# Layer 0 of a four-layer graph network: engine order from a list of steps run through at build time, far entries scaled on ScalarE

## Chip, cores, metric

One core of a Trainium2 chip runs the whole program in one launch. The metric is device time in microseconds (us). The engines are named as in the profile: PE (TensorE, with PEld for its weight loads), DVE (VectorE), ACT (ScalarE), POOL (GpSimd), SP (SyncE, which here only issues transfers).

## The reference, cut to what matters

Four graph layers run one after the other on 2708 nodes with 128 features, each with a residual and a normalisation. The change concerns layer 0 only.

```
# node_feats: x [2708,128]; adj [2708,2708], about 64 entries per row not zero, in 0.05..1
s = x @ msg_w[:, :128].T
d = x @ msg_w[:, 128:].T
messages   = gelu(s[:, None, :] + d[None, :, :] + msg_b)      # exact gelu
aggregated = einsum('ijd,ij->id', messages, adj)
new = concat([x, aggregated]) @ upd_w.T + upd_b
h   = gelu(new) + x
x   = layernorm(x + (layernorm(h) * ln_w + ln_b))
# layers 1 to 3 follow, each a layernorm(x + layer(x, adj))
```

The gelu of a pair (i, j) is wanted only where `adj[i, j]` is not zero. The kernel computes it at those places alone.

## The kernel before, in words

**Tiles and blocks.** The 2708 rows are taken in 22 row tiles (`LT`) of 125 rows (`LR`, five groups of `RG` = 25). For each tile the 2708 columns are 22 blocks (`NB`) of 124 columns (`JB`). So there are 484 blocks, and a block is the unit in which everything is ordered.

**A block.** `begin` (L953) puts the rows' s into the PSUM buffer `sl`, for two blocks at a time. `pick` (L960, ten matmuls) adds, for each row and each of five slots, the d of one neighbour in this block; the same matmul brings that neighbour's adjacency value. A slot matrix `S` (one in the place of the neighbour that has this rank in its row and block) makes the choice. `CAP` = 5 slots hold the first five entries of a row in a block. ACT takes the gelu into `g` (L1042), DVE spreads the adjacency values into `W` (`weigh`, L1026), and `add_up` (L977) multiplies `W` by `g` into the PSUM buffer `acc`. There are three `sl`, six `g` and six `W`.

**Preparing a tile.** For each third of the columns: SP loads the adjacency transposed (`at`, L808/L811), DVE makes a mask (`find`, L817), PE ranks (L825) and ACT casts the ranks (L826); ACT and DVE split the adjacency values into two FP16 parts `dA` (L833, L838), and DVE writes five slots (`slot`, L845).

**Far entries.** A row may have more than five entries in a block. Those past the cap are called far, at most `OV` = 16 a row. SP loads the adjacency by rows (`ar`, L860). PE ranks along rows (L866); DVE keeps the entries past the cap in `o` (`past`, L877), counts them (L879), takes the eight largest of every two blocks (L884) and of those the sixteen largest `v` (L890, L892). FIND_INDEX8 (`where`, L915) finds their columns, twice eight. SP fills a buffer `far` of 128x8x128 with the rows' s, 512 KB (`start_far`, L910); POOL gathers onto it the d of one column per row, eight times (`fetch`, L919, an indirect transfer that adds). ACT takes the gelu of the buffer (`far_gelu`, L925). DVE sums the sixteen with their values, one after the other (`far_sum`, L931, then fifteen of L933). `turn` (L939 to L942, PE) adds this to the tile's sums, `close` (L945, ACT) stores it. There are three `far` buffers. `check` (L899 to L906, eight small DVE operations a tile) compares the count of entries past the cap with the number of values found, and looks for equal values, [...]; a total ends up in an output.

**Order.** Within this stage the order of each engine's instructions is the order in which the program issues them. It is written out by hand: `preparation` and `Rows.when` (from L753) name for every step the block after which it comes, the list of steps is sorted by block, and one loop over the 484 blocks (L1032 to L1053) issues the steps between the blocks. For the far part these lines say it:

```
b = base + NB
yield b, self.largest
yield b + 6, self.check
for n in range(OV // 8):
    yield b + 1 + n * 2, lambda n=n: self.where(n)
...
    yield b - 1 + n * 9, lambda n=n: self.start_far(n)
    yield b + 2 + n * 9, lambda n=n: self.fetch(n)
    yield b + 15 + n * 13, lambda n=n: self.far_gelu(n)
    for k in range(8):
        yield b + 17 + n * 13 + k // 2, lambda n=n, k=k: self.far_sum(n * 8 + k)
yield b + 36, self.turn
yield b + 36, self.close
```

Here `b` is the first block of the tile. An engine takes its instructions in that order and waits on semaphores for what others make. Buffers come from tile pools, so a buffer's next use waits for the last use of the one before. After the last block (L1056 to L1094) the update of the features follows, with the rest of the last tile's far entries between its groups.

Of the kernel before, what the change touches and what calls it, by code (L numbers as in the profile page):

```python
# [14 lines left out]
F32 = mybir.dt.float32  # L15
# [7 lines left out]
P = 128  # L23
# [47 lines left out]
class Step:  # L71


    def __init__(self, engine, cost, emit, after, rank, group, ahead, table, cells, bank, then):
        self.engine, self.cost, self.emit, self.after, self.rank = engine, cost, emit, after, rank
        self.group, self.ahead, self.table, self.cells, self.bank, self.then = group, ahead, table, cells, bank, then
        self.end = None

# [94 lines left out]
def gnn_stack(ctx: ExitStack, tc: tile.TileContext, t, out: bass.AP):  # L173
# [378 lines left out]
    with ExitStack() as l0:  # L552
# [10 lines left out]
        with ExitStack() as msg:  # L563
# [28 lines left out]
            nc.vector.memset(spread, 0.0)  # L592
# [4 lines left out]
            nc.vector.tensor_copy(spread[:, :, :RG], ident[:, :LR].rearrange("p (c i) -> p c i", c=NC))  # L597

            bad = mp.tile([P, LT], F32, name="bad")
# [3 lines left out]
            with tc.tile_pool(name="pre0", bufs=1) as pp:  # L603
                trif = pp.tile([JB, P], F32, name="trif")
                nc.vector.memset(trif, 1.0)
                nc.gpsimd.affine_select(
                    out=trif[:, :JB], in_=trif[:, :JB], compare_op=ALU.is_gt, fill=0.0, base=0,
                    pattern=[[1, JB]], channel_multiplier=-1)
                nc.vector.scalar_tensor_tensor(
                    trif[:, :JB], ident[:JB, :JB], EDGE, trif[:, :JB], op0=ALU.mult, op1=ALU.add)  # L610
                nc.vector.tensor_copy(tri, trif)


# [11 lines left out]
            lp = msg.enter_context(tc.tile_pool(name="load", bufs=3))  # L625
            ap_ = msg.enter_context(tc.tile_pool(name="rowsof", bufs=3))
            mk = msg.enter_context(tc.tile_pool(name="masks", bufs=2))
            sp = msg.enter_context(tc.tile_pool(name="ranks", bufs=3))
            op_ = msg.enter_context(tc.tile_pool(name="past", bufs=1))
            gp = msg.enter_context(tc.tile_pool(name="fetch", bufs=3))  # L630
            vp = msg.enter_context(tc.tile_pool(name="values", bufs=3))
            up = msg.enter_context(tc.tile_pool(name="sums", bufs=2))
            ep = msg.enter_context(tc.tile_pool(name="slots", bufs=6))
            p_misc = msg.enter_context(tc.tile_pool(name="ps_misc", bufs=1, space=PSUM))
            p_slot = msg.enter_context(tc.tile_pool(name="ps_slot", bufs=1, space=PSUM))
            p_out = msg.enter_context(tc.tile_pool(name="ps_out", bufs=1, space=PSUM))
            sl_all = [p_slot.tile([P, 2, BANK], F32, name=f"sl{n}") for n in range(3)]
            for v in sl_all:
                nc.vector.memset(v, 0.0)
# [7 lines left out]
            xT = aggT  # L647

            def turn_x():
                for n, (a, b) in enumerate(spans(0, NT, 4)):  # L650
                    ps = sl_all[n % 3][:, n // 3, :]
                    for i in range(a, b):
                        r = rows[i]
                        nc.tensor.transpose(ps[:, (i - a) * P:(i - a) * P + r], x[:r, i, :], ident[:r, :r])
                    w = min(b * P, N) - a * P
                    (nc.scalar.copy if n % 2 else nc.vector.tensor_copy)(xT[:, a * P:a * P + w], ps[:, :w])

            class Piece:


                def __init__(self, n):
                    self.n = n
                    self.b0, self.b1 = 4 * n, min(4 * n + 4, NB)
                    self.a0, self.a1 = 4 * n, min(4 * n + 4, NT)

                def products(self):
                    b0, b1, a0, a1 = self.b0, self.b1, self.a0, self.a1
                    psd, pss = (sl_all[(2 * self.n + k) % 3][:, 0, :].rearrange("p (b d) -> p b d", d=D)
                                for k in range(2))
                    d = self.d = ep.tile([P, NC, D], F32, name="g")[:JB, :b1 - b0, :]  # L670
                    room = gp.tile([P, 8, D], F32, name="far")
                    s = self.s = room[:, :a1 - a0, :]
                    parts = room[:, 4:, :].rearrange("p i d -> p (i d)").bitcast(FP16)
                    self.parts = parts.rearrange("p (q i d) -> p q i d", q=2, d=D)[:, :, :a1 - a0, :]
                    if N < b1 * JB:
                        nc.vector.memset(d, 0.0)
                    if N < a1 * P:
                        nc.vector.memset(s, 0.0)
                    for b in range(b0, b1):
                        r = min(JB, N - b * JB)  # L680
                        nc.tensor.matmul(psd[:r, b - b0, :], xT[:, b * JB:b * JB + r], msg_d, start=True, stop=True)
                    for i in range(a0, a1):
                        nc.tensor.matmul(pss[:rows[i], i - a0, :], xT[:, i * P:i * P + rows[i]], msg_s,
                                         start=True, stop=True)
                    full = min(b1, NFB) - b0
# [4 lines left out]
                    self.hi, self.lo = (v[:, b0:b1, :, :D] for v in dA)  # L690
                    nc.scalar.activation(self.hi[:, :, 0, :], d, AF.Copy, scale=D_SCALE)
                    self.spread(self.hi)
                    for a, b, r in groups():
                        if a0 <= a < a1:
                            nc.vector.tensor_tensor(s[:r, a - a0:b - a0, :], pss[:r, a - a0:b - a0, :],
                                                    over_tiles(msg_br, b - a, r), op=ALU.add)
                    nc.scalar.activation(self.parts[:, 0], s, AF.Copy, scale=D_SCALE)
                    nc.sync.dma_start(out=s_tab[a0 * P:a1 * P, :].rearrange("(n p) d -> p n d", p=P), in_=s)
# [4 lines left out]
                def spread(self, v):  # L703

                    nc.gpsimd.tensor_copy(v[:, :, 1:, :], v[:, :, 0:1, :].to_broadcast(
                        [JB, self.b1 - self.b0, NC - 1, D]))

                def update(self):
                    ps = p_out.tile([P, PB, D], F32, name="acc")
                    u = ep.tile([P, NC, D], F32, name="g")[:, :self.a1 - self.a0, :]  # L710
                    if N < self.a1 * P:
                        nc.vector.memset(u, 0.0)
                    for a, b, r in groups():
                        if self.a0 <= a < self.a1:
                            for i in range(a, b):
                                nc.tensor.matmul(ps[:r, i - self.a0, :], xT[:, i * P:i * P + r], upd_x,
                                                 start=True, stop=True)
                            nc.vector.tensor_tensor(u[:r, a - self.a0:b - self.a0, :],
                                                    ps[:r, a - self.a0:b - self.a0, :],
                                                    over_tiles(upd_b, b - a, r), op=ALU.add)  # L720
                    nc.sync.dma_start(out=u_tab[self.a0 * P:self.a1 * P, :].rearrange("(n p) d -> p n d", p=P), in_=u)

                def rests(self):
                    b0, b1, a0, a1 = self.b0, self.b1, self.a0, self.a1
                    lo = self.lo
                    nc.vector.scalar_tensor_tensor(self.parts[:, 1], self.s, D_SCALE, self.parts[:, 0], op0=ALU.mult,
                                                   op1=ALU.subtract)
                    nc.vector.scalar_tensor_tensor(lo[:, :, 0, :], self.d, D_SCALE, self.hi[:, :, 0, :], op0=ALU.mult,
                                                   op1=ALU.subtract)
                    self.spread(lo)  # L730
                    for q in range(2):
                        nc.sync.dma_start(out=sq_tab[q, a0 * P:a1 * P, :].rearrange("(n p) d -> p n d", p=P),
                                          in_=self.parts[:, q])

            def preparation():
                yield -NB - 9, turn_x
                for n, b in enumerate((-26, -22, -14, -10, -6, -2)):
                    piece = Piece(n)
                    yield b, piece.products
                    yield b + 2, piece.update  # L740
# [1219 lines left out]
```

## Time and profile before

| | |
|---|---|
| median of 3 runs | 1880.69 us (1878.36 to 1881.56) |
| the profiled execution's own time | 1879.03 us |
| span in the profile | 1877.3 us |
| mean granted TensorE clock | 0.920 |
| layer 0: first gelu of a block, last one | 55.5 us, 855.7 us |
| end of layer 0 | about 897.5 us |
| one row tile in the middle | 36.03 to 36.05 us |

The times of the runs are device times of whole executions. Everything with a line number, a window or an engine comes from the one profiled execution. A row of the groups reads: line, engine, operation, written tile, read tiles, shapes, count, then busy us in all, mean ns of one, and the idle time before it with what ended it. A row of waits reads: who waited, for whom, us in total, times, longest us. In a timeline the columns are start, duration, engine, line, operation, and in brackets the idle time before it.

### The profile page before, as it was taken

Reading aid. Unit: us, or ns where it says so; the run is one execution under the profiler, and the core shown is the slowest. Engines: PE = TensorE matmul, PEld = TensorE weight load, DVE = VectorE, ACT = ScalarE, POOL = GpSimd, SP = SyncE. Lnnn points to the kernel's source line nnn. Section 1 sums busy time; section 2 is a strip of 40 time slices with the busy share of each in tenths; the row PEclk is TensorE's granted clock in tenths of the full one; section 3 lists DMA queues with packets and bytes.
Section 4 is the critical chain, followed back from the end, with each engine's and each line's share of the span. In section 5 each row is a group of like instructions: output and inputs, shape, how many; then the busy total and the mean of one; then the engine's idle time right before and its main releaser. Section 6 shows DMA issues by size and latency. Waiting matters only on the chain.

```text
span 1877.3 us, 36661 instructions
## 1 busy us (share of the span) xinstructions
PE 1581.1 (84%) x14033; PEld 921.2 (49%) x14033; DVE 1432.4 (76%) x3609; ACT 999.4 (53%) x1538; POOL 653.2 (35%) x429
## 2 busy tenths in 40 slices
PE   4889999999999999884799995568888897299995
PEld 4666666666666666663444442312322343044542
DVE  7899999999999999976588885748886782860104
ACT  3556666666666666544344443568886862430003
POOL 5667767777777776664100000010000100000000
PEclk9899999999999999997899998658997798599998
DMA  8757666666666766543044410032333554354431
GB/s 223 167 117 153 127 144 145 135 145 128 147 135 137 151 129 139 101 104 104 0 154 161 164 64 1 9 118 89 139 139 117 171 174 169 118 207 148 148 123 32
DMA packets 234895, 238.29 MB, mean 127 GB/s; under 512 B 28844, under 2 KB 219630, under 8 KB 228122
## 3 DMA queue, kind: packets, MB, share of 16 engines
q1 hardware_dynamic: 183670, 212.18, 36.2%
q0 software_dynamic: 51040, 23.68, 10.6%
q8 instruction: 112, 1.84, 0.4%
q14 instruction: 73, 0.60, 0.1%
HBM read 220.65 MB, written 15.15 MB: 126 GB/s over the span
## 4 chain that ended last, share of the span: by engine, by line
PE 38%; DVE 7%; ACT 6%; issue 1%; DMA 0%; ACTq 0%; DVEq 0%
PE acc L1857 11%; PE lg L1245 5%; PE acc L1252 5%; PE accV L1585 5%; PE ps L1513 4%; PE accO L1589 2%; PE ps L1568 1%; ACT arena L1519 1%; DVE arena L1547 1%; PE ps L1514 1%; ACT x L379 1%; DVE arena L1571 1%; PE ps L447 1%; PE ps_w L1213 1%; ACT arena L1540 0%
## 5 line engine op out<-in xcount | busy, mean ns | idle before, releaser
L919 POOL DMA_INDIRECT far<-d_tab,ix x352 | 583.1, 1657 | 217.3 <-issue 97.0
L1042 ACT ACTIVATE g<-sl 128x640 f32<-128x640 f32 x484 | 335.4, 703 | 297.3 <-PE sl L960 272.5
L960 PE MATMUL sl<-dA,S 124*128 124x153 f16 x4840 | 380.9, 233 | 0.0
L960 PEld LDWEIGHTS <-S 124*128 124x128 f16 x4840 | 326.0, 98 | 72.0 <-issue 69.8
L977 PE MATMUL acc<-g,W 128*32 128x128 f32 x4840 | 194.5, 280 | 15.5 <-DVE W L1026 13.5
L953 PE MATMUL sl<-s,same 50*128 50x459 f16 x968 | 150.5, 333 | 17.8 <-DVE W L1026 15.5
L977 PEld LDWEIGHTS acc<-g,W 128*32 128x32 f32 x4840 | 117.4, 109 | 70.4 <-DVE W L1026 27.5
L1026 DVE TENSOR_TENSOR W<-sl,own 128x125 f32<-128x125 f32 x484 | 131.2, 275 | 21.6 <-ACT g L1042 21.6
L1500 POOL TENSOR_TENSOR arena<-arena,off 128x128 f32<-128x128 f32 (+1 forms) x22 | 23.0, 1049 | 350.3 <-DMA arena<-in_adjT 245.1
L845 DVE TENSOR_SCALAR S<-rk 124x1000 f16<-124x1000 bf16 (+1 forms) x330 | 141.4, 455 | 0.0
L1246 ACT ACTIVATE w<-lg,row_L_gnn_gate_bias 128x512 f32<-128x512 f32 (+1 forms) x132 | 83.4, 636 | 108.2 <-PE lg L1245 107.0
L915 DVE FIND_INDEX8 ix<-v,o 128x8 uint32<-128x2728 f32 x44 | 131.8, 2994 | 0.0
L1585 PE MATMUL accV<-arena,X 128*128 128x512 f32 (+4 forms) x264 | 123.3, 587 | 6.5 <-DVE arena L1551 6.5
L1245 PE MATMUL lg<-qT,mT 128*128 128x512 f32 (+2 forms) x264 | 121.2, 548 | 3.6 <-ACT w L1246 3.1
L1252 PE MATMUL acc<-w,both 128*128 128x512 f32 (+2 forms) x264 | 121.2, 547 | 0.0
L449 DVE TENSOR_TENSOR g<-ps,row_L_gnn_b 128x512 f32<-128x512 f32 (+2 forms) x14 | 7.9, 573 | 147.4 <-PE ps L447 147.3
L933 DVE SCALAR_TENSOR_TENSOR extra<-far,v,extra 128x128 f32<-128x128 f32 x330 | 114.6, 347 | 6.8 <-ACT far L925 0.5
L1513 PE MATMUL ps<-XT 128*128 128x512 f32 (+8 forms) x150 | 91.0, 696 | 32.2 <-ACT arena L1519 26.5
L1857 PE MATMUL acc<-at,x 128*128 128x512 f32 (+2 forms) x156 | 66.2, 575 | 48.5 <-ACT x L379 48.5
L1247 DVE TENSOR_TENSOR w<-w,at 128x512 f32<-128x512 f32 (+1 forms) x132 | 82.6, 626 | 27.1 <-ACT w L1246 27.0
L877 DVE SCALAR_TENSOR_TENSOR o<-ps,ar 128x496 f32<-128x496 f32 x132 | 82.0, 621 | 12.2 <-DMA ar<-in_adj 6.8
L884 DVE MAX8 cand<-o 128x8 f32<-128x248 f32 x242 | 90.4, 412 | 0.0
(359 smaller groups left out, 2494.2 us busy)
## 6 DMA issues: line engine op xcount, KB each, us to landing
at<-in_adjT SPq DMA_DIRECT2D x42, 1354.0 KB
ar<-in_adj SPq DMA_DIRECT2D x105, 248.0 KB
far<-s_tab SPq DMA_DIRECT2D x44, 512.0 KB
at<-in_adjT SPq DMA_DIRECT2D x42, 448.0 KB
arena<-in_adjT SPq DMA_DIRECT2D x21, 704.0 KB
arena<-in_adjT SPq DMA_DIRECT2D x21, 650.0 KB
held<-in_adjT SPq DMA_DIRECT2D x7, 1354.0 KB
f_tab<-arena SPq DMA_DIRECT2D x10, 704.0 KB
```

Of the source, the lines that this page charges most:

```text
L845: nc.vector.tensor_scalar(self.S[h][:, :n, :, k * RG:(k + 1) * RG], self.rk[h][:, :n, :LR].rearrange("p b (c i) -> p b c i", c=NC), EDGE + ...
L915: nc.vector.max_index(ix, self.v[:, n * 8:n * 8 + 8], self.o.rearrange("p b j -> p (b j)"))
L919: nc.gpsimd.indirect_dma_start(out=self.far[n][:, k, :], out_offset=None, in_=d_tab[:, :], in_offset=bass.IndirectOffsetOnAxis(ap=self.ix[ ...
L953: nc.tensor.matmul(columns_of(sl, 0, DA)[:, a:e, :], same[p], self.s3[p, :e - a, :], start=True, stop=False)
L960: nc.tensor.matmul(columns_of(sl, 0, DA)[:, c, :], self.S[h][:, n, c, :], dA[q][:, b, c, :], start=False, stop=q == 1 and c in (2, NC - 1))
L977: nc.tensor.matmul(self.acc[q:q + 32, k, :], W[:, c, :], g[:, c, :], start=b == 0 and k == 0, stop=ends)
L1042: nc.scalar.activation(g, columns_of(sl, 0, D), AF.Gelu, scale=1.0 / D_SCALE)
L1245: nc.tensor.matmul(lg, mT[:, j * P:j * P + r], qT[:, a:b], start=True, stop=True)
L1252: nc.tensor.matmul(acc[k], mrow[:rows[j], j, :], ws[j][:rows[j], a:b], start=j == 0, stop=j == NT - 1)
L1513: nc.tensor.matmul(ps, XT[:, self.js], XT[:, c], start=True, stop=False)
L1585: nc.tensor.matmul(Pair.acc[0][:, a:b], X[:self.r, self.j, :], self.w_[:, a:b], start=first, stop=last)
L1857: nc.tensor.matmul(acc[k], src[:rows[j], j, :], at[:rows[j], a:b], start=j == order[0], stop=j == order[-1])
```

## The change

The computation stays; order, buffers and the place of some operations change.

- A new class `Order` holds a list of steps. Each has an engine, a price in us that is written beside it, what it reads and writes, a number `due` (in blocks) and, for some, a lag until the result can be used. Going through the list at build time, `run` lets the free engine with the smallest `due` among its ready steps go next, and issues the instructions in that order. The table `DUE` takes the place of the hand-written block numbers; no step is tied to a block any more except through `due` and through what it reads and writes.
- All buffers of the stage are made once and taken in turn: `at`, `ar`, `rk`, `far`, `ix` three each, `mask` two, `g` six, `extra` and `cand` two, `agg` one (two before). The clearing of `at` and `ar` moves to POOL, once, at the start.
- The far entries are multiplied by their values on ACT (`far_weigh`, sixteen activations with a scale pointer), and the sixteen products are summed on DVE by halving (`far_sums`, four additions of 1024, 512, 256 and 128 columns), in place of the sixteen chained operations.
- The count of entries past the cap is copied by ACT (six a tile, from the PSUM buffer that `past` reads); the check is made once, over all tiles, by nine DVE operations near the end of the stage.
- In the last tile the second eight scalings and the four additions stand after the third group of the update, as the far sums did.

The diff, cut to its core:

```diff
+class Order:
+    LATENCY, TURN = 0.12, 0.1
+    def add(self, engine, cost, emit, due, reads=(), writes=(), lag=0.0, take=None, give=None, kind=None):
...
+    def run(self, buffers):
...
+            for e, mine in ready.items():
+                if free_at.get(e, 0.0) > now:
+                    continue
...
+                    end = now + s.cost + self.TURN * (s.kind != kinds.get(e, s.kind))
...
+                    s.emit()
...
+                        a.ready = max(a.ready, end if a.engine == e else end + s.lag + self.LATENCY)
...
+            DUE = {"load": -24, "load_s": -34, "load_row": 60, "start_far": 30,
+                   "rank": -20, "rank_row": -18.5, "begin": -0.3, "pick": 0, "add_up": 2.5, "turn": 10,
+                   "out": -40, "count": -99, "cast": -3.5, "a_hi": -3.5, "gelu": 13.5, "far_weigh": 32, "close": 80,
+                   "far_gelu": 90, "weigh": -50, "largest": -36, "index": -35, "mask": -15, "far_sum": -15,
+                   "past": -14, "max": -6, "a_lo": -2.5, "S": -2, "fetch": 0}
...
-                def far_sum(self, k):
-                    w, f = self.v[:, k:k + 1], self.far[k // 8][:, k % 8, :]
-                    if k == 0:
-                        self.extra = up.tile([P, D], F32, name="extra")
-                        nc.vector.tensor_scalar(self.extra, f, w, None, op0=ALU.mult)
-                    else:
-                        nc.vector.scalar_tensor_tensor(self.extra, f, w, self.extra, op0=ALU.mult, op1=ALU.add)
...
+                            add("POOL", 1.56, fetch, due + DUE["fetch"] + k,
+                                reads=[("ix", f), ("far", f), *(("d_tab", j) for j in range(6))],
+                                writes=[("far", f, k)], lag=2.5)
...
+                    add("ACT", 0.95, lambda: self.far_gelu(n), due + DUE["far_gelu"], reads=[("far", f)], writes=each)
+                    for k in range(8):
+                        add("ACT", 0.29, lambda k=k: self.far_weigh(n, k), due + DUE["far_weigh"] + k / 2, reads=[("far", f)],
+                            writes=[("far", f, k)])
...
+                def far_weigh(self, n, k):
+                    f = far_all[(self.t * (OV // 8) + n) % 3][:, k, :]
+                    nc.scalar.activation(f, f, AF.Copy, scale=self.v[:, n * 8 + k:n * 8 + k + 1])
...
+                    yield "DVE", 1.12, plus(a, a, b), keys[1], keys[0]
+                    yield "DVE", 0.63, plus(a[:, :4, :], a[:, :4, :], a[:, 4:, :]), (), keys[0]
+                    yield "DVE", 0.37, plus(a[:, :2, :], a[:, :2, :], a[:, 2:4, :]), (), keys[0]
+                    yield "DVE", 0.26, plus(self.extra, a[:, 0, :], a[:, 1, :]), keys[0], [("extra", self.t % 2)]
...
-                    yield b + 6, self.check
...
+                    add("ACT", 0.15, lambda: nc.scalar.copy(count_all[:, t, b], misc[:, :n, JB]), due + DUE["count"],
+                        reads=[one], writes=[("count", t, m)], give=("misc", one, 2))
...
+            add_check((LT - 1) * NB + 8)
+            with tc.manual_schedule():
+                order.run({"misc": 1})
```

## The prediction

> **What bounds the kernel now.** I read the busy rows and the slices of the page first. The change touches layer 0 alone, which fills the first 897 us.
>
> ```profile
> PE 1581.1 (84%) x14033; PEld 921.2 (49%) x14033; DVE 1432.4 (76%) x3609; ACT 999.4 (53%) x1538; POOL 653.2 (35%) x429
> ...
> PE   4889999999999999884799995568888897299995
> ...
> DVE  7899999999999999976588885748886782860104
> ```
>
> The whole-span shares hide the stage: in slices 3 to 17 (from about 94 to 845 us) PE and DVE both stand at 9. So I asked for busy times by window: one row tile in the middle, the last blocks of layer 0, and what follows them.
>
> ```profile
> core 0: us, PE busy (x) PEld busy (x) DVE busy (x) ACT busy (x) POOL busy (x), PEclk, DMA share, GB/s
> 306.00:342.00 36.00, 33.49 (x518) 24.08 (x518) 34.90 (x101) 22.99 (x38) 26.63 (x17) 1.00 0.65 140
> ...
> 840.00:860.00 20.00, 19.89 (x317) 15.39 (x314) 9.93 (x33) 10.74 (x20) 16.67 (x11) 1.00 0.48 79
> ...
> 856.40:897.50 41.10, 10.08 (x80) 7.95 (x72) 28.90 (x104) 18.47 (x42) 10.98 (x11) 0.60 0.30 107
> ```
>
> A tile lasts 36.0 us (gelu of its first block to the next tile's, 36.03 to 36.05). DVE works 34.9 of it, the fullest engine. Where DVE has little to do (second row), PE takes 317 matmuls in 20 us; the 518 to 520 of a tile at that pace are 20/317 x 520 = 32.8 us: PE's floor. PE's waits from 100 to 800 us (columns: us in total, times, longest us) show the link:
>
> ```profile
> ACT g L1042 <- PE sl L960: 237.8, 220, 3.1
> POOL far L919 <- issue: 87.2, 286, 0.3
> ...
> PE sl L953 <- DVE W L1026: 14.7, 40, 0.9
> PE ps L866 <- DVE count L879: 14.3, 19, 0.8
> ...
> PE acc L977 <- DVE W L1026: 10.1, 22, 0.9
> ...
> PE ps L825 <- DVE mask L817: 7.6, 19, 0.5
> ```
>
> The last four sum to 46.7 us in 19.4 tiles, 2.4 us a tile: the weighing of a block and the counts come late on DVE. ACT only waits for PE. So layer 0 is bound by DVE, with PE 3 us beneath.
>
> POOL is the third clock. In the last tile the second eight gathers can be followed alone:
>
> ```profile
> 827.31 2.99 DVE L915 FIND_INDEX8 ix<-v,o 128x8 uint32<-128x2728 f32 x1
> ...
> 858.91 1.55 POOL L919 DMA_INDIRECT far<-d_tab,ix  x1 [0.30 <-issue]
> 863.16 1.06 ACT L925 ACTIVATE far<-far 128x1024 f32<-128x1024 f32 x1 [2.35 <-DMA far<-d_tab,ix]
> ```
>
> Each gather takes 1.55 + 0.30 = 1.85 us, so sixteen take 29.7 us a tile, and the last lands 863.16 - 858.91 = 4.25 us after it starts (view of the tile far: 3.2/4.2/6.7 us).
>
> [...] 1.55 us shown, 4.25 us to landing. Hence the loop below takes the landing. [...]
>
> **The change, part by part.**
>
> *DVE in a tile.* Removed: the chained far sums. The page has 330 of L933 at 347 ns, 15 a tile: 5.2 us; the first (L931) adds 0.3. The check (eight small operations, 1.1 us in a timeline), six counts (L879, 150 ns: 0.9) and the repeated memsets (0.2) go too. Together -7.7. Added: four additions of 1024, 512, 256 and 128 columns. [...] the trace agrees at 1024 (L1551, 1218 ns). That is 1.22 + 0.69 + 0.42 + 0.28 = 2.6, and two or three hand-overs from ACT at 0.1, 0.2. Net -4.9: DVE 34.9 to 30.0.
>
> *ACT in a tile.* Added: sixteen scalings with a pointer for scale. [...] L1407 of the trace, the same operation, shows 385, 292 apart. 16 x 0.29 = 4.7; six counts copied, at 0.16 to 0.2 each (the 150 ns of L879 as nearest row), 1.1. ACT goes from 23.0 to 28.8: room left.
>
> *PE and POOL* keep their work: 32.8 and 29.7 us. So the fullest is PE, and what the order adds decides.
>
> *The far loop.* In the built order SP issues two refills of 512 KB back to back, after DVE has added the two far buffers: the next tile's first half, then this pair's other buffer for its second half. Three buffers turn; in before the refills stand apart. The second half of a tile then runs: refill landed 5.0 us after issue (the packets of L910's queue end 3.5 to 4.5 us after it; both ends 4.5 and 7.4, as two now share the queue), seven further gathers 7 x 1.85 = 13.0, landing 4.2, gelu 1.05, eight scalings 2.3, and on ACT between them five gelus of blocks (0.60 to 0.68), a cast 0.5, a count 0.15 and one adjacency scaling 1.0, together 4.9; then the first additions with waits, 3.1. Sum 33.5; with 0.2 for two semaphores **33.7 us** (32.5 to 35.5). It passes PE's 32.8. A tile bound by DVE at 34.9 took 1.1 more; I add 0.8 of that: **34.5 us** a tile (33.3 to 35.6).
>
> *Waits added.* ACT takes instructions in order: behind a far gelu that waits for gathers stand the gelus of coming blocks, for which PE waits after three PSUM buffers. The change plans a gather at 1.56, not 1.85, so this wait appears; it is inside the loop. Behind SP's two refills stand the next adjacency rows, due most of a tile later: nothing. The single small PSUM buffer is now freed by ACT's count and DVE; between 0.3 lost and 0.5 gained a tile, taken as 0.
>
> *Start.* In before the first gelu starts at 55.5 us, the first weighing at 58.0; from 16 to 55.5 us DVE works 35.6. The built order puts some 45 of its operations from then on ahead of the first weighing: the bias additions and remainders of six pieces (18), three masks, three of six searches for entries past the cap, one third's slots and adjacency remainder. At the durations of before's timeline (0.69 for 512 columns, 0.68 a mask, 0.65 + 0.74 for a search, 0.42 a slot, 1.2 for the adjacency remainder, and two remainders at the 1.36 and 2.18 that they took there) they come to 27 us. With gaps of 6 (the trace has 4 between 16 and 32 us; I allow 2 more, as the pieces follow closer) that is 16 + 27 + 6 = 49: -6.5 (-10 to -1). Tiles 0 and 1, 36.2 and 39.2 us, lose 3.4 in all (-5 to -1).
>
> *Middle.* From tile 2 to 20, 18 tiles: 18 x (36.05 - 34.5) = -28 (-8 to -49). From 20 to 21 the gap is 44.8 us, since the last tile's rows on 83 partitions load slowly; [...] The trace agrees (packets one by one, 84 ns apart). This stays: -1.5.
>
> *Tail.* The last index search stands two blocks later against the end; the gathers behind it are the path, and eight scalings (2.3) precede 2.6 of additions where 3.06 stood: +4 (0 to +7). The nine operations of the single check lie beside the last gathers; without that cover 4 us. Last tile's blocks: 0.
>
> Sum: -6.5 - 3.4 - 28 - 1.5 + 4 = **-35.4**. The profiled execution took 1879.03 (span 1877.3), so 1843.6; the median of the runs stands 1.7 above it: **1845**. The main case's own range, with the ends of the terms, is 1824 to 1871.
>
> **Rivals.**
>
> *The far loop has slack, PE is the bound.* For it: PE reached 32.8 near the end, and the first half has time. A tile is 33.2: 18 x 2.85 = -51; with start, first tiles, gap and tail -58 to -62: about 1820. Against it: the waits on gathers in order.
>
> *Slower: ACT's queue held by gathers.* It decides once the loop exceeds 36.05, 2.3 over 33.7: if the pair of refills lands at 7.4 instead of 5.0, or gathers slow to 2.15. At 36.9 a tile: +15, start and first tiles -6, tail +4: about 1894. For it: three buffers, a gather priced too low, and a far gelu ahead of five block gelus. Against it: the packets seen end at 4.5, not 7.4, and PE still has up to three blocks in hand.
>
> *No gain.* The loop stands near 36 and the tail takes what the start gives: 1877 to 1884.
>
> *The change does not do what it says.* Excluded: the built order shows sixteen scalings on ACT and four additions on DVE per tile.
>
> **How the numbers follow.** Main case 0.60, PE-bound 0.20, no gain 0.06, slower 0.14. Faster is the first two, 0.80. A measurement of this kernel can tell about 0.2%, 3.8 us. Range 1812 to 1884: it leaves out the slower case and a little below.
>
> **What would show it.** Right: DVE about 30 of 34.5 us in a middle tile, ACT near 29; PE's waits for DVE under 1 us a tile; idle before far gelus ended by a far gather; POOL idle before its first gather ended by SP's refill; first gelu near 49. Wrong in a step: PE busy nearly all of a 33 us tile (loop slack); the additions waiting on scalings for several us; ACT idle on gathers over 3 us a tile, and tiles over 36 us.

## The result, and the profile after

The changed kernel takes 1949.0 us (median of 4 runs, 1942.2 to 1956.6), the kernel before 1880.6: ratio 1.0367, 95% interval 1.0318 to 1.0415. It is slower by 68 us where 36 less were forecast. The profiled execution took 1954.19 us (span 1952.5). Its page, part 1 and three slice rows:

```profile
PE 1596.6 (82%) x14033; PEld 940.1 (48%) x14033; DVE 1366.5 (70%) x2997; ACT 1105.4 (57%) x2022; POOL 655.7 (34%) x433
...
PE   5888988888888888887189999368888899099995
...
DVE  8787878787787788884758886765797683770104
ACT  3477777766776777674434443467887772430103
```

DVE did lose work (1432 to 1367 us in all, 612 instructions fewer) and ACT took it (999 to 1105). But PE, DVE and ACT now stand at 8, 8 and 7 through layer 0: nothing is full. The windows view shows one middle tile, and then the middle of the stage (columns as before):

```profile
301.30:339.50 38.20, 33.53 (x522) 24.48 (x520) 31.20 (x75) 27.73 (x60) 26.05 (x16) 1.00 0.63 135
130.00:780.00 650.00, 572.87 (x8684) 417.43 (x8685) 522.77 (x1202) 467.72 (x1012) 443.26 (x267) 0.97 0.61 128
```

A tile takes 38.2 us with DVE at 31.2, PE at 33.5 and ACT at 27.7: the tile waits. The waits from 100 to 800 us say on whom:

```profile
DVE W L1127 <- ACT g L147: 98.0, 113, 4.1
...
PE sl L1102 <- DVE W L1127: 32.9, 40, 3.4
PE sl L1102 <- ACT g L147: 29.2, 20, 3.5
ACT far L1023 <- DMA far<-d_tab,ix: 27.8, 13, 3.7
...
ACT far L1023 <- issue: 21.0, 9, 3.0
...
ACT far L1023 <- DMA ar<-in_adj: 7.3, 7, 2.3
```

Before, DVE made PE wait. Now ACT makes DVE and PE wait, and ACT itself waits at L1023, the far gelu, 56 us in all (the last row's name is a guess of the view; that instruction waits for its gathers alone).

Where the 75.2 us between the two profiled spans went, from the starts of the block gelus:

| | before | after | difference | forecast |
|---|---|---|---|---|
| first gelu | 55.5 | 56.8 | +1.3 | -6.5 |
| tiles 0 and 1 | 75.4 | 82.4 | +7.0 | -3.4 |
| tiles 2 to 19, 18 tiles | 36.08 each | 38.91 each | +51.0 | -28 |
| tile 20 (the gap) | 44.8 | 40.0 | -4.8 | -1.5 |
| last tile, to its last gelu | 30.6 | 44.4 | +13.8 | 0 |
| all after it | 1021.6 | 1028.4 | +6.8 | +4 |

### The profile page after: what moved, and what is told of

It reads as the page before. It is cut to its first block, busy times and chain, and to the rows that moved or that the text cites. A ratio compares the mean times of both kernels' runs of the same rounds, so it can differ in the third digit from the quotient of the medians.

```text
span 1952.5 us, 36369 instructions
## 1 busy us (share of the span) xinstructions
PE 1596.6 (82%) x14033; PEld 940.1 (48%) x14033; DVE 1366.5 (70%) x2997; ACT 1105.4 (57%) x2022; POOL 655.7 (34%) x433
## 5 line engine op out<-in xcount | busy, mean ns | idle before, releaser
L1110 PE MATMUL sl<-dA,S 124*128 124x153 f16 x4840 | 405.1, 237 | 0.1
L1110 PEld LDWEIGHTS <-S 124*128 124x128 f16 x4840 | 341.6, 101 | 74.9 <-issue 67.4
L1118 PE MATMUL acc<-g,W 128*32 128x128 f32 x4840 | 188.6, 282 | 0.2 <-ACT g L147 0.2
L1118 PEld LDWEIGHTS acc<-g,W 128*32 128x32 f32 x4840 | 121.9, 111 | 45.1 <-issue 24.6
L1646 POOL TENSOR_TENSOR arena<-arena,off 128x128 f32<-128x128 f32 (+1 forms) x22 | 20.8, 944 | 352.1 <-DMA arena<-in_adjT 282.1
L913 DVE TENSOR_SCALAR S<-rk 124x1000 f16<-124x1000 bf16 (+1 forms) x330 | 127.9, 424 | 0.0
L1027 ACT ACTIVATE far<-far,v 128x128 f32<-128x128 f32 x352 | 126.1, 401 | 0.7
L1102 PEld LDWEIGHTS <-same 50*128 50x128 f16 x968 | 39.0, 94 | 152.8 <-issue 147.1
L1393 DVE TENSOR_TENSOR w<-w,at 128x512 f32<-128x512 f32 (+1 forms) x132 | 82.4, 625 | 27.2 <-ACT w L1392 27.2
L908 DVE SCALAR_TENSOR_TENSOR dA<-at,dA 124x1000 f16<-124x1000 f32 (+1 forms) x66 | 72.5, 1098 | 28.6 <-ACT dA L906 28.5
```

Source lines behind the costliest of these rows:

```text
L1102: nc.tensor.matmul(columns_of(sl, 0, DA)[:, a:e, :], same[p], self.s3[p, :e - a, :], start=True, stop=False)
L1110: nc.tensor.matmul(columns_of(sl, 0, DA)[:, c, :], S_all[h][:, n, c, :], dA[q][:, b, c, :], start=False, stop=q == 1 and c in (2, NC - 1))
L1118: nc.tensor.matmul(acc_all[q:q + 32, k, :], W_all[W][:, c, :], g_all[g][:, c, :], start=b == 0 and k == 0, stop=ends)
```

## The experiments

"PE gaps" below are worked out from the matmul records of tiles 3 to 18: the time from the end of one to the start of the next where it is over 0.25 us, per tile. Before has 2.1 us, the changed kernel 4.3, of which 1.4 at the seventh block of a tile and 1.6 at the nineteenth: a few blocks behind the two far gelus, for in the order the second far gelu of a tile stands behind the fourth block of the next tile and the first behind the sixteenth. "Tile" is the mean of tiles 2 to 19, from the starts of their first block gelus. Each ratio is taken against runs of the kernel before made beside the kernel in question (medians of 1880.4 to 1881.3 us).

| kernel | median us | ratio to before, interval | tile us | PE gaps us |
|---|---|---|---|---|
| before | 1880.6 | | 36.08 | 2.1 |
| changed | 1949.0 | 1.0367 (1.0318 to 1.0415) | 38.91 | 4.3 |
| x1_far4 | 1991.7 | 1.0588 (1.0555 to 1.0621) | 41.35 | 5.3 |
| x2_swap | 1995.1 | 1.0597 (1.0578 to 1.0616) | 41.43 | 5.4 |
| x3_halves | 1974.1 | 1.0493 (1.0474 to 1.0512) | 41.22 | 5.2 |
| x12_far4_same | 1950.8 | 1.0346 (1.0290 to 1.0401) | 38.60 | 4.0 |
| x6_prices | 1902.8 | 1.0112 (1.0085 to 1.0139) | 36.44 | 2.5 |
| x7_far4_prices | 1905.3 | 1.0133 (1.0100 to 1.0166) | 36.73 | 3.0 |
| y1_half | 1873.6 | 0.9975 (0.9959 to 0.9990) | 35.97 | 2.0 |
| x10_chain_prices | 1889.9 | 1.0047 (1.0033 to 1.0062) | 36.40 | 2.4 |
| x4_hand | 1898.7 | 1.0090 (1.0072 to 1.0108) | 37.02 | 3.2 |
| x8_hand_spread | 1949.5 | 1.0376 (1.0349 to 1.0402) | 39.65 | 4.4 |
| x11_hand_place | 1935.9 | 1.0307 (1.0279 to 1.0335) | 38.82 | 3.6 |
| x9_counts | 1869.3 | 0.9931 (0.9913 to 0.9949) | 35.25 | 1.8 |
| y2_even | 1940.4 | 1.0312 (1.0289 to 1.0335) | 38.87 | 4.2 |
| y3_act | 1949.4 | 1.0368 (1.0351 to 1.0385) | 38.65 | 4.2 |
| y4_best | 1861.8 | 0.9893 (0.9877 to 0.9910) | 35.25 | 1.8 |
| y5_best1 | 1873.9 | 0.9963 (0.9949 to 0.9977) | 35.93 | 1.8 |
| y6_list | 1878.0 | 0.9993 (0.9977 to 1.0010) | 35.94 | 1.9 |

### Is it the ring of far buffers? x1, x2, x3

The prediction's far loop is a ring: a far buffer is filled, gathered onto, summed, and only then filled again, so no tile can be shorter than one round. With the measured terms the round came to 38.0 us. That looked like the answer, so the first three kernels open that ring.

```diff
-            far_all, ix_all = several(3, [P, 8, D], F32, "far"), several(3, [P, 8], U32, "ix")
+            far_all, ix_all = several(4, [P, 8, D], F32, "far"), several(4, [P, 8], U32, "ix")
# and % 3 to % 4 where far_all is taken
```

> The changed kernel with four far buffers instead of three (the third-third's at, rk and S buffers are cut to the 6 blocks they use, to make room; no step is added or removed). Theory ring: the tile of 38 to 40 us is the ring of one buffer: refill issued 6.4 us before the first gather, seven gathers 13.8, landing 5.1, gelu 1.06, scalings among block gelus 8.8, four additions 2.9, sum 38. With four buffers a refill has a whole tile of slack, the ring is gone, and PE or POOL sets 34 to 36 us a tile: 20 tiles x 3 to 4 less, time 1870 to 1890. Rival queue: ACT's fixed order, planned with gathers of 1.56 us, makes block gelus wait behind far gelus whatever the buffers: 1940 to 1957 as the changed kernel.

```diff
-                    a, b = (far_all[f] for f in fars)
-                    keys = [... for f in fars]
+                    b, a = (far_all[f] for f in fars)
+                    keys = [... for f in reversed(fars)]
```

> The changed kernel with the two far buffers added into the second instead of the first, so that the buffer which the next tile's second half needs is freed by the first addition and refilled first (not after the three shorter additions and not behind another 512 KB). Theory ring: the ring loses 1.6 us of additions and 1 to 1.5 us of refill: 35.5 to 36 us a tile, 20 x 2.5 less, 1890 to 1915. Rival queue: 1940 to 1957.

```diff
-                    yield "DVE", 1.12, plus(a, a, b), keys[1], keys[0]
+                    for n, (f, key) in enumerate(zip(fars, keys)):      # each half: 512, 256, 128 columns
...
```

> The changed kernel with each half of the far entries halved by itself (512, 256, 128 columns) and then added, so that the first half's buffer comes free some 17 blocks before the second's. DVE pays 0.4 us a tile more. Theory ring: the ring is cut as with a fourth buffer: 34 to 36.5 us a tile, 1870 to 1895. Rival queue: 1940 to 1957.

All three are slower than the changed kernel: 1992, 1995 and 1974 us, tiles of 41.2 to 41.4. Neither theory had that. The order differs: with a buffer free sooner, the list puts the second half's far gelu after 24 block gelus (x3, later in the stage, 22) instead of 26, counted from the start of the tile. The timeline of x1, at the start of a tile:

```profile
348.81 1.06 ACT L1024 ACTIVATE far<-far 128x1024 f32<-128x1024 f32 x1 [4.86 <-issue]
...
349.97 0.38 PE L891 MATMUL misc<-mask,tri 124*128 124x512 bf16 x1 [4.31 <-ACT count L937]
...
350.56 0.29 DVE L1128 TENSOR_TENSOR W<-sl,own 128x125 f32<-128x125 f32 x1 [5.52 <-ACT g L147]
...
351.89 2.99 DVE L987 FIND_INDEX8 ix<-v,o 128x8 uint32<-128x2728 f32 x1
```

ACT waits 4.9 us for the gathers. Behind it in ACT's queue stands a count copy that frees the one small PSUM buffer, so PE's next rank waits 4.3 us in PE's queue; behind that rank stand the picks of new blocks, so DVE waits 5.5; and behind DVE's weighings stands the next tile's index search, which starts the next gathers. From one first search (310.51) to this far gelu are 38.3 us, from there to the next search 3.1: 41.4, the tile. The ring is closed by the queues, in blocks, not by a buffer.

The changed kernel has the same chain. From two answers of its timeline:

```profile
301.32 3.00 DVE L986 FIND_INDEX8 ix<-v,o 128x8 uint32<-128x2728 f32 x1
...
305.04 1.54 POOL L997 DMA_INDIRECT far<-d_tab,ix  x1 [4.92 <-ACT far L1023]
...
322.90 1.54 POOL L997 DMA_INDIRECT far<-d_tab,ix  x1 [2.92 <-DVE W L1127]
...
336.73 1.55 POOL L997 DMA_INDIRECT far<-d_tab,ix  x1 [0.30 <-ACT count L936]
...
339.47 2.99 DVE L986 FIND_INDEX8 ix<-v,o 128x8 uint32<-128x2728 f32 x1
...
341.45 1.06 ACT L1023 ACTIVATE far<-far 128x1024 f32<-128x1024 f32 x1 [2.15 <-issue]
```

Search 3.0, hand-over 0.7, first eight gathers 14.9, wait 2.9, to the start of the sixteenth 13.8, landing 4.7: 40.1 us from search to far gelu. In the order these stand 22 blocks apart (search after 4 weighings, far gelu after 26 block gelus), and 22 blocks, one tile, last 36.1 us at the pace of before. Before has 28 blocks there (1 and 29): 45.9 us at that pace, and its far gelus do not wait in tiles 3 to 18.

The first half is as tight. From the same search to the first far gelu are 22.8 us in this tile, and the order gives it 12 blocks (4 and 16), 19.7 us at the pace of before, which has 15 there. Over tiles 3 to 18 the first far gelu of a tile waits 1.5 us on average and the second 1.6.

### The same order on four buffers: x5, x12

> Four far buffers in the chip's memory, but the list run through with three, so that every engine's order stays that of the changed kernel (far gelu of the second half after 26 block gelus, where the earlier four-buffer kernel had 24). Theory ring: a free buffer takes the refill out of the ring of 38 us; the tile falls to 35.5 to 36.5, 1890 to 1905. Theory queue alone (the buffers have nothing to do): unchanged, 1940 to 1957.

x5 was badly made. In the order the refill for the tile after next stands ahead of the three shorter additions, and with four buffers it fell on the buffer being added; DVE waited 60 us for it, and the sums were then of the wrong rows. Its 2027.6 us say nothing. x12 adds into the other buffer.

```diff
-                    a, b = (far_all[f] for f in fars)
+                    a, b = (far_all[(2 * self.t + 1 - n) % 4] for n in range(2))
```

> The order of the changed kernel, step for step, on four far buffers, now with the two buffers added into the one that the order leaves alone (in the earlier try the refill that the order puts ahead of the three shorter additions fell on the buffer still being summed). Theory ring: 35.5 to 37 us a tile and a shorter last tile, 1885 to 1915. Theory queue alone: tiles as before, 38.5 to 39.5, only the last tile shorter: 1925 to 1957.

38.6 us a tile: the buffers are not what sets it. The fourth buffer did come free: the wait ahead of the second eight gathers falls from 2.0 us a tile on average to 0.8. ACT's waits at the far gelu from 130 to 780 us nearly all stay, 44.4 us in x12 for 50.5 in the changed kernel:

```profile
ACT far L1024 <- DMA far<-d_tab,ix: 23.6, 13, 3.5
ACT far L1024 <- issue: 12.4, 7, 2.6
...
ACT far L1024 <- DMA ar<-in_adj: 8.4, 8, 2.2
```

The last tile did not get shorter (43.9 us), so that part of the expectation failed.

### True prices, and gathers left out: x6, x7, y1

```diff
-                            add("POOL", 1.56, fetch, ...   lag=2.5)
+                            add("POOL", 1.9, fetch, ...    lag=3.2)
# and lag=6.4 instead of 5.0 for the refill
```

> The changed kernel with three numbers of the list set to what the traces show: a gather at 1.9 us, its landing 3.2 later, a refill landing after 6.4. The order puts the far gelus after 18 and 30 block gelus instead of 16 and 26; three buffers stay. Theory ring: the buffer ring of 38 us does not care for where the far gelu stands: 1935 to 1960. Theory queue: ACT no longer waits in front of block gelus, 34 to 36 us a tile: 1860 to 1895.

> Both: four far buffers and the three measured numbers; far gelus after 18 and 28 block gelus. If ring and queue are two rings that take each other's place, only this one is free of both: 33.5 to 35.5 us a tile, 1850 to 1880. If ACT's load with the scalings is the cause, 37 us a tile and more stays: 1905 or more.

Three numbers in the list take 46 us off (1949 to 1903), with three buffers: 36.4 us a tile, a little above what the theory of the queue gave. A fourth buffer adds nothing (x7: 36.7 us a tile, between its two expectations). ACT's waits from 130 to 780 us in x6, with the first row for comparison of size:

```profile
ACT g L147 <- PE sl L1110: 74.3, 89, 1.9
...
ACT far L1023 <- DMA far<-d_tab,ix: 16.8, 13, 2.8
...
ACT far L1023 <- DMA ar<-in_adj: 3.8, 4, 1.5
...
ACT far L1023 <- issue: 0.2, 1, 0.2
```

20.8 us at the far gelu; the changed kernel has 50.5 in that window. All of the 20.8 stands at the first far gelus, 14 blocks behind their search; the second ones, now 26 blocks behind it, do not wait. But x6 also moves other steps. y1 moves none: it keeps the changed order and makes the gathers fewer.

```diff
                             def fetch(k=k, far=far, ix=ix):
+                                if k >= 4:
+                                    return
```

> The changed kernel with its order kept step for step, and four of the eight gathers of each half left out (their far entries are not added; everything else is as it was). Nothing but the time until the gathers have landed changes: a set takes 7.4 us less. Theory queue (ACT's far gelu stands too few blocks after the index search for eight gathers at 1.87 us): ACT no longer waits in front of block gelus, PE's gaps of 1.4 and 1.6 us behind the far gelus go, 35.5 to 36.8 us a tile, 1885 to 1915. Theory load (sixteen scalings and two far gelus are simply too much between the block gelus): 38.0 to 39 us a tile, 1930 to 1957.

35.97 us a tile, and no wait at all at the far gelu (35.7 us from search to second far gelu, for 22 blocks); the whole time, 1873.6, is below what was expected, as the first two and the last two tiles are shorter too. Fewer gathers also shorten the ring of buffers and halve the gathers' traffic. x12 speaks against the ring, and x6, which keeps every gather, against the traffic. So the three together show it: with every other step in its place, the stall comes and goes with the time that the gathers take, measured against the blocks that the order leaves them. That is 2.9 us a tile and some 50 of the 68 us. y1 also shows what was left to win: with no such wait the changed kernel's tile is still 36.0, as before's. The windows of before and of y1:

```profile
130.00:780.00 650.00, 604.33 (x9334) 434.71 (x9333) 630.24 (x1805) 413.84 (x684) 480.54 (x288) 1.00 0.65 138
```

```profile
130.00:780.00 650.00, 604.61 (x9376) 439.50 (x9372) 558.83 (x1304) 503.28 (x1085) 240.12 (x144) 1.00 0.53 124
```

In y1 DVE is at 86% (97% in before) and PE at 93%, as in before. 4 us less DVE work a tile, and nothing gained.

### Scalings on ACT, with and without the new order: x10, x4, x8, x11

x10 is x6 with the scalings undone: sixteen chained multiply-adds on DVE again.

> The changed kernel with the three measured numbers, and the scalings on ACT undone: sixteen chained multiply-adds on DVE again, each far buffer free after its own eight. If ACT's sixteen scalings cost time in the new order (they are the rest of what the three numbers left, 36.4 us a tile): 35.5 us a tile or less, 1860 to 1890. If DVE's load rules: 36.5 to 37.5, 1905 to 1925.

Its tile of 36.4 equals x6's; towards the end of the stage it runs at 35.7. Neither expectation is met clearly: in the tile ACT's sixteen scalings and DVE's sixteen additions cost about the same. The whole time is 13 us less than x6's (17.5 in the profiled executions); most of that lies in the first two tiles (4.4 us) and the last two (10.9).

x4 takes before's hand-written order, and only the scalings and the halving:

```diff
-                        for k in range(8):
-                            yield b + 17 + n * 13 + k // 2, lambda n=n, k=k: self.far_sum(n * 8 + k)
+                        for k in range(8):
+                            yield b + 16 + n * 13 + k // 2, lambda n=n, k=k: self.far_weigh(n, k)
+                        yield b + 20 + n * 13, lambda n=n: self.far_sum(n)      # halves one far buffer
```

> The kernel before with its hand-written order kept, and only this part of the change: sixteen scalings on ACT (from the block after each far gelu, two a block) and each half summed by halving on DVE four blocks after its gelu. DVE loses 5.5 and gains 3.1 us a tile. If scaling on ACT is sound and the loss comes from the order and its buffers: 34 to 34.8 us a tile, 1840 to 1860. Rival load: sixteen more activations among the gelus hold up the blocks themselves: 1880 or more.

Slower than before: 37.0 us a tile with DVE at 33.6 (589.9 of 650 us). Two rows of its waits from 150 to 770 us:

```profile
DVE dA L839 <- ACT dA L834: 35.4, 34, 1.2
...
PE ps L826 <- ACT rk L827: 17.2, 17, 1.0
```

The scalings stand in front of adjacency parts and rank casts, which DVE and PE wait for: 3 us of waits a tile that before does not have. Two attempts to place them better failed:

> The kernel with the hand-written order and the scalings on ACT (37.0 us a tile), the scalings now one a block instead of two, sums five blocks later, turn and close four later. If two scalings a block held back the rank casts and adjacency parts that DVE and PE wait for (in that trace DVE waited 2.1 us a tile for L834, PE 1.0 for L827): 35 to 36 us a tile, 1860 to 1885. If the load of ACT as such is the cause, 36.9 stays: 1895 to 1900.

> The kernel with the hand-written order and the scalings on ACT (37.0 us a tile), far gelus and scalings moved to blocks in which ACT has no rank cast and no adjacency part: far gelu at block offsets 18 and 33 (was 15 and 28), two scalings a block behind it, sums at 27 and 38, turn and close at 40. If it was the place of the scalings: 35 to 36, 1860 to 1885. If the load as such: 36.9 and more, 1895 or more.

Both moved the sums too, and PE then waited for DVE's weighings behind searches and sums (gaps of 2.0 and 1.7 us a tile in x8, of 1.9 in x11). They say that the place of a step matters by 2 to 3 us a tile; whether a place exists at which the scalings cost nothing stays open.

### The other part alone, and the edges: x9, y2, y3

```diff
-                    nc.vector.tensor_scalar(self.count[:, b], self.ps[m][:, :n, JB], -float(CAP), 0.0, ...)
+                    nc.scalar.copy(count_all[:, self.t, b], self.ps[m][:, :n, JB])
-                    yield b + 6, self.check          # and one check over all tiles, once
```

> The kernel before with only the counts and the check of the change: six counts a tile copied by ACT instead of computed by DVE, one check at the end instead of one a tile (the third S buffer is cut to the blocks it uses, to make room). DVE loses 0.9 + 1.1 us a tile, ACT gains 1.1. If before is bound by DVE's busy time, as the prediction had it: 34 to 35 us a tile, 1845 to 1865. If the tile is set by hand-overs in fixed queues, and not by DVE's busy time: within 0.5 us of 36.0, 1870 to 1890.

This side part of the change is the one that pays: 35.2 us a tile, 0.7% faster. The tile is 0.8 us shorter, of which PE's gaps are 0.3. At 35.2 it lies between the two expectations, and what in this part brings the gain was not separated: DVE works 1.6 us a tile less, but PE still waits for the counts, now ACT's.

```diff
-                    nc.sync.dma_start(out=...[:self.r, :n_in], in_=adj[self.r0:self.r0 + self.r, ...])
+                    for p0, p1 in even(self.r):          # 83 rows: 80 and 3
+                        nc.sync.dma_start(out=...[p0:p1, :n_in], in_=adj[self.r0 + p0:self.r0 + p1, ...])
```

> The changed kernel with the adjacency rows of the last tile, 83 partitions, loaded as 80 and 3 (every other tile has 128 and is untouched). If the refill of tile 20's second half lands late because it waits behind these rows (ACT waited 13 us there), the last two tiles lose 10 to 14 us: 1932 to 1942. If not: 1942 to 1957.

The last two tiles fall from 84.4 to 70.7 us, the expected 14; the whole time by 9, since its tail took 1.6 longer and the runs scatter. In the changed kernel's trace the place looks like this:

```profile
880.33 1.57 POOL L997 DMA_INDIRECT far<-d_tab,ix  x1 [16.64 <-ACT rk L893]
```

```profile
897.67 1.06 ACT L1023 ACTIVATE far<-far 128x1024 f32<-128x1024 f32 x1 [12.96 <-DMA far<-d_tab,ix]
```

POOL stands for 16.6 us because the refill is behind loads of 83 rows in SP's queue, and ACT, in order, then stands for 13. In y2 the same two waits are 0.3 and 2.9 us.

```diff
-                    nc.gpsimd.tensor_copy(v[:, :, 1:, :], v[:, :, 0:1, :].to_broadcast(...))
+                    nc.scalar.copy(v[:, :, 1:, :], v[:, :, 0:1, :].to_broadcast(...))
```

> The changed kernel with the twelve copies that spread d over five groups made by ACT instead of POOL (preparation only; ACT is idle for most of it). If DVE's ten remainders took 1.95 us each instead of 0.68 because POOL copied at the same time, they fall back to 0.7, and the first gelu comes at 47 to 52 us instead of 56.8: 4 to 10 us less, 1936 to 1946. If not: first gelu 56 or later.

One half holds, one fails. The remainders' row, first in the changed kernel, then in y3:

```profile
L844 DVE SCALAR_TENSOR_TENSOR dA<-g,dA x6: 1184/1948/2382, 18.2 to 44.4; 124x512 f16<-124x512 f32 x5, 124x256 f16<-124x256 f32 x1
```

```profile
L844 DVE SCALAR_TENSOR_TENSOR dA<-g,dA x6: 430/684/696, 17.1 to 49.1; 124x512 f16<-124x512 f32 x5, 124x256 f16<-124x256 f32 x1
```

1.95 us falls to 0.68 once POOL no longer copies. But ACT's twelve copies of 1.9 us then are the chain, and the first gelu comes at 61.3.

### Putting together: y4, y5, y6

y4 is x9 with y2's loads. y5 adds to it the scalings of the second half. y6 is the changed kernel with x6's numbers, PE's prices as measured, y2's loads and y3's copies.

> The kernel with the hand-written order and only counts and check changed (1869.3 us, 35.2 a tile), and the last tile's rows loaded as 80 and 3 partitions. The gap of 44.8 us from tile 20 to 21 should fall to about 36 as it did in the changed kernel (last two tiles together 84.4 to 70.7 there): 1856 to 1864. If in this order the rows were not what the gap waited for: 1865 to 1870.

> The same, and the second half's far entries scaled on ACT and halved on DVE (two scalings a block, blocks 29 to 32, a block after its far gelu), the first half chained on DVE as before. DVE loses another 1.1 us a tile, ACT gains 2.3. If DVE's busy time still rules: 34.2 to 34.8 a tile, 1840 to 1855. If ACT's share in the block loop weighs as much as DVE's: 35 to 35.8, 1855 to 1875.

> The changed kernel with the three measured numbers, PE's prices as the traces show them (a pick 0.76, a begin 0.28, a sum matmul 0.04 us), the last tile's rows as 80 and 3, and the spread copies on ACT. If the list needs only true prices: 34 to 35.5 us a tile, 1840 to 1870. If ACT's scalings keep costing what DVE gained: 36 to 37, 1880 to 1900.

y4 beats both kernels: 1861.8 us, 1.1% below before. y5 is 12 us slower than y4: it takes only 0.5 us a tile off DVE, not the 1.1 expected, and adds 2.1 to ACT, and the tile is 0.7 us longer. y6 ends level with before, at 35.9 us a tile between its two expectations.

## Why the prediction was wrong, step by step

- **What the change moves: right.** DVE was put at 30.0 and ACT at 28.8 us a tile; y1, which runs without the stall, has 30.9 and 27.9 (window shares times 35.97). In the changed kernel the four additions take 1215, 699, 414 and 282 ns (L1035, mean of 22 each), where the prediction has 1.22, 0.69, 0.42 and 0.28 us; before's trace has 1218, 692, 419 and 283 ns for DVE operations of these widths (L1551, L1248, L1571). A scaling takes 401 ns (L1027), and four in a row 1.28 us, a step of 0.29 each.
- **"It is inside the loop": the step that failed.** The prediction saw that the plan prices a gather at 1.56 and pays 1.85, that ACT then waits, and that block gelus stand behind. It took this as covered by the ring of three buffers, which it set at 33.7. It never counted blocks: from the search 12 to the first far gelu, against a chain of 22.8 us, and 22 to the second, against 40.1 us. At 34.5 us a tile these blocks last 18.8 and 34.5 us. So the wait had to come outside the ring: 3.0 us a tile at the far gelus. x12 shows that the buffers hardly matter, y1 and x6 that this wait does. The rival on the slower side named this mechanism and gave it 0.14 and 36.9 us a tile; measured are 38.9.
- **Terms of the chain, each too small.** In the tile shown, refill to first gather 6.4 for 5.0, landing 4.7 for 4.2, ACT's stretch from the end of the gelu to the additions 8.8 for 7.2. They fed a ring that does not bind, yet the same gathers and landings lie on the one that does.
- **PE's floor 32.8, "DVE-bound".** The 20 us window from which it came has no searches or far entries of a later tile. In no kernel here is a tile without its gaps below 33.4 us, and none has less than 1.8 us of gaps. By this count only some 2 us a tile stood to be won by a saving on DVE; x9 got 0.8.
- **Middle: -28 forecast, +51 measured.** 18 x 2.83. Of the 2.83, 2.2 are PE gaps (4.3 - 2.1); the other 0.6 is PE taking longer between them (see the last section).
- **Start: -6.5 forecast, +1.3.** The remainders were priced at 0.68 except two, as in before, where the twelve take 9.9 us in all; in the changed kernel they take 22.0, and in y3, where POOL does not copy, 7.6. That this alone moved the first gelu is not shown, since in y3 ACT's copies delay it. Tiles 0 and 1: two gelus waited 5.2 us for stores of u out of the buffers that they write; that was read, not tested.
- **Last tile: 0 forecast, +13.8; gap -1.5, -4.8.** The slow loads of the last tile's 83 rows (packets one by one, 84 ns apart, in before) were seen and called unchanged; why they are slow is not shown by a run here. What was behind them in the queue had changed: the refill of tile 20's second half (y2).
- **Tail: +4 forecast, +6.8 measured.** Within the term's range.

## What to carry to other kernels

Where engines take instructions in a fixed order, an instruction that waits for a long transfer has to stand as many blocks behind its start as the transfer takes at the pace wanted: 22 blocks last 36.1 us at the pace of before; the second far gelu waited 2.15 us where search to far gelu took 40.1 us (changed, the tile shown) and not at all where it took 35.7 (y1). Count those blocks in the order and multiply before looking at any engine's busy time. Here a list scheduler turned a gather's price that was a sixth too low (1.56 for 1.85 us) and two landings that were a quarter too low (2.5 for 3.2, 5.0 for 6.4) into a stall on every tile, so take its prices from a trace of the kernel, landing included, and check with a run that leaves the transfer out. The busy share of the fullest engine did not say what moving its work would bring: DVE at 97% in before and 86% in y1 goes with tiles of 36.08 and 35.97 us. PE's gaps, 2.1 and 2.0 us a tile there, did not shrink either.

## What the runs showed of the hardware that was not expected

DVE's remainders took longer while POOL copied. Those of L844 have a median of 1.95 us in the changed kernel, where POOL makes the copies, and 0.68 in y3, where ACT makes them. In before the two that met a copy of POOL's took 1.36 and 2.18 us (L726, at 18.73 and 23.26 us), the other ten 0.41 to 0.69 (L726, L728).

The granted clock was lower in the kernels with the most gaps of PE. From 130 to 780 us it is 1.00 at 2.1 us of gaps a tile (before), 0.97 at 4.3 (changed) and 0.93 at 5.3 (x1). The tile without its gaps is longer where the clock is lower: 34.0, 34.6 and 36.0 us. In that window of the changed kernel the trace's records of the clock show half of it in ten stretches, 34 us in all, and each begins within 7 us of a single gap of 1.9 us or more. Seven of its seventeen gaps of 1.4 us and more bring none. Before, whose longest gap is 0.8 us, has no such stretch, and x4, with 3.2 us of gaps a tile, has a clock of 1.00 as well. No run changed the gaps alone, so it is not shown that the gaps lower the clock.

Loading 83 rows as 80 and 3 took the gap from tile 20 to 21 from 44.8 to 38.2 us in the hand-written order (x9 to y4).
